# Which PSUM banks take the score maxima made first in a step: the two single banks instead of the pair

## The chip, the cores and the metric

The kernel runs on one core of a Trainium2 chip. The metric is the device time of one execution in microseconds (us). Engines are named as in the profile: PE (TensorE matmuls), PEld (TensorE weight loads), DVE (VectorE), ACT (ScalarE), POOL (GpSimd), SP (SyncE, which issues the DMAs).

## The reference

`x` is (8, 512, 1024). An attention block over the 512 channels (16 heads of 32, 1024 tokens, a mask over the keys from `cond_2048`) is followed by a linear layer on int8 values with one scale for each row, and the result is added to `x`:

```python
Q, K, V = (proj(Wq), proj(Wk), proj(Wv))          # einsum 'oc,bct->bto', then split into heads
att = einsum('bhqd,bhkd->bhqk', Q, K) / sqrt(32) + b[0]
att = softmax(att * m + (1 - m) * -1e30)          # m: mask of the keys
y = einsum('bhqk,bhkd->bhqd', att, V)             # back to (B, C, T)
scale = maximum(max(abs(y), axis=-1), 1e-7) / 127
q = clip(round(y / scale), -128, 127)             # int8
out = (q @ weight.T) * scale * w_scale + bias     # stored as float16
return x + out
```

All inputs but the int8 weight are float32.

## The kernel before, in words

The work is cut into 32 groups `i` (8 batches, 4 groups of 4 heads). A group is 16 steps: two halves of 512 queries, and in each half 8 blocks of 128 keys. So there are 512 steps `s`, with `t = s % 16`, after a prologue of 11 steps with negative numbers (`LEAD = 11`). The order of every engine's instructions is written out by hand (`tc.manual_schedule`); nothing is moved by a scheduler.

PSUM has eight banks of 512 float32 columns: four single ones, `one[0]` to `one[3]`, and two pairs, `two[0]` and `two[1]`, which an engine can read as 1024 columns in one instruction.

A step with `s >= 0` issues on PE, in this order:

1. `shift_scores(s)`, L338: four bf16 products that put minus the row maxima into the four banks of scores: two single banks and the pair `two[1]`. Even steps use `one[0]` and `one[1]`, odd steps `one[2]` and `one[3]`; from step 501 (`TAIL`) on it differs.
2. `scores(s, (0, 1))`, L348: the scores of heads 0 and 1, added to the single banks. Each head has 32 rows, so four heads can lie side by side on the array. The operands are float32, and a product is two passes.
3. `maxima(m, ..., (1, 0))`, L282, for step `m = s + 11`, that is 11 steps ahead: scores laid the other way round (128 queries by 512 keys), of which only the maximum over the keys is kept. Two heads are done in a step, each in two halves of the keys, so four products. The second half (`turn`) uses copies of q and k with neighbouring heads exchanged (`qt`, `kt`, made by DMA), so that the two halves of a head lie in two different row groups. Head 1 of the list is made first, head 0 second.
4. `scores(s, (2, 3))`, L348: the scores of heads 2 and 3, in `two[1]`.
5. In even steps `product` (L380): the exponentials of the last two steps times v, over the full height of the array, into the first single bank of this step's scores once the exponentials have been read from it. Its result is taken by ACT (L390) or DVE (L392).
6. The step's pieces of other work (`plan`): in even steps a 128-column piece of v for the next group (L186, kept by ACT, L267) in the second single bank of the scores; in odd steps two of a linear layer's half (kept by DVE, L525), a piece of q or k (kept by ACT, L220 and L222) and half a block of denominators (L398, kept by ACT, L405), one in each single bank of the scores. The last one is in the second bank.

`take_maxima` (L302) is DVE's part: it adds the mask row and takes the maximum, in one instruction over 1024 columns where a head's two halves lie in a pair, in two over 512 where they lie in two single banks; each is followed by the read of an accumulator (DVE_READ_ACCUMULATOR2, also L302). ACT turns the scores into exponentials (L362): two instructions for the single banks, one for the pair. POOL adds the exponentials up (L372).

`maxima_banks(s)` says which banks the two heads of the maxima get. For `s >= 0` these are the two single banks that the scores of this step do not use (so those that the step before filled with scores, then with its product and pieces, and that the next step's L338 writes), and the pair `two[0]`, which nothing else uses. The list's place 0 is head 0, its place 1 head 1; both `maxima` and `take_maxima` are called with `(1, 0)`, so place 1 comes first on PE and on DVE.

Of the kernel before, what the change touches and what calls it, by code (L numbers as in the profile page):

```python
# [33 lines left out]
def kernel(  # L34
# [44 lines left out]
    one = [psum.tile([P, HALF], F32, tag=f"one{a}", name=f"one{a}") for a in range(4)]  # L79
    two = [psum.tile([P, NH, HALF], F32, tag=f"two{a}", name=f"two{a}") for a in range(2)]  # L80

    def halves(t):
        return [t[:, a, :] for a in range(NH)]
# [5 lines left out]
    def maxima_banks(s):  # L89
        if s < 0:  # L90
            turns = (halves(two[0]), halves(two[1]), one[:2])
            return [turns[(2 * s + a) % 3] for a in range(2)]
        return [one[2:] if s % 2 == 0 else one[:2], halves(two[0])]

    x_sb = {}

# [611 lines left out]
    for s in range(-LEAD, n_steps):  # L708
# [36 lines left out]
        if s < 0:  # L745
            multiply()
            keep(False)
            maxima(m, maxima_banks(s))
            take_maxima(m, maxima_banks(s), range(2))
        else:  # L750

            shift_scores(s)
            scores(s, (0, 1))
            if m < n_steps:
                maxima(m, maxima_banks(s), (1, 0))
                take_maxima(m, maxima_banks(s), (1, 0))
            scores(s, (2, 3))
            exponentials(s)
            add_up(s)
            if s >= TAIL:  # L760
                for a in range(ON_ARRAY if s == TAIL + 1 else s - 1, s if s > TAIL else 0):
                    late(a)
            elif s > 0 and s % 2 == 0:
                acc = score_banks(s)[0][0]
                for a in (2, 1):
                    product(s - a, acc, a == 2, a == 1)
                keep_product((s - 2) // NT, (s - 2) % NT == 0, acc)
            multiply()
            keep(True)
# [68 lines left out]
```

## Time and profile before

| | |
|---|---|
| median of 3 runs | 2472.9 us (2472.07 to 2475.49) |
| the profiled execution | 2474.28 us, span 2472.5 us, mean granted clock 0.996 |
| PE busy | 2443.9 us, 99% |
| DVE busy | 1831.0 us, 74% |
| ACT busy | 1557.1 us, 63% |
| POOL busy | 2293.4 us, 93% |
| L282, products into `one` and into `two` | 2036 and 2060 passes, 589 ns each |
| L302 over 1024 columns | 515, 1225 ns each |
| L302 over 512 columns | 509 at 691 ns and 509 at 751 ns |
| one step in the middle | 4.81 us (even), 4.58 us (odd) |

The profile is one execution, with times in us from the start of the span. A matmul's end is modelled, so "busy" on PE covers passes that lie side by side, and also a step in which one of the row groups waits while another works. The list of waits names the waiting engine and line, then the one it waited for, with the total in us, the number of times and the longest.

### The profile page before, as it was taken

The numbers are of one execution on the slowest core, as the hardware profiler recorded it, in microseconds if no ns is written. First come the engines' busy times: TensorE is split into PE (matmuls) and PEld (weight loads), VectorE is DVE, ScalarE is ACT, GpSimd is POOL, SyncE is SP. The second block draws the span as 40 slices with busy tenths as digits, with TensorE's granted clock in tenths as the row PEclk, the third lists the DMA queues.
The fourth block names the chain that finished last, engine by engine and source line by source line (L and its number), as shares of the span: only waits on it lengthen the run. The fifth ranks groups of instructions, "written<-read, shape, count | busy, mean of one in ns | idle before, by whom it ended". The sixth has DMA issues, their size and how long they took to land.

```text
span 2472.5 us, 82389 instructions
## 1 busy us (share of the span) xinstructions
PE 2443.9 (99%) x35496; PEld 1156.9 (47%) x35496; DVE 1831.0 (74%) x3769; ACT 1557.1 (63%) x2382; POOL 2293.4 (93%) x961
## 2 busy tenths in 40 slices
PE   9999999999999999999999999999999999999987
PEld 4444444444444444444444444444444444444432
DVE  5677777777777777777777777777777777777774
ACT  1666666666666666666566676666665666666664
POOL 0999999999999999999999999999999999999992
PEclk9999999999999999999999999999999999999999
DMA  4013111121211211122111211112211122111111
GB/s 127 21 32 83 42 40 35 42 80 45 47 38 38 72 49 45 38 53 64 40 45 47 53 57 40 47 45 56 69 30 40 49 68 58 34 41 40 36 29 50
DMA packets 146590, 121.49 MB, mean 49 GB/s; under 512 B 77872, under 2 KB 111664, under 8 KB 146224
## 3 DMA queue, kind: packets, MB, share of 16 engines
q1 hardware_dynamic: 146224, 116.22, 17.8%
q8 instruction: 278, 4.55, 0.8%
q14 instruction: 88, 0.72, 0.1%
HBM read 57.70 MB, written 16.78 MB: 30 GB/s over the span
## 4 chain that ended last, share of the span: by engine, by line
PE 96%; DVE 2%; issue 0%; DMA 0%; ACT 0%; POOL 0%; SPq 0%; DVEq 0%; POOLq 0%
PE one L186 32%; PE one L380 19%; PE one L348 17%; PE one L282 17%; PE one L338 7%; PE one L398 3%; DVE rest L302 2%; PE two L282 1%; PE two L348 0%; DMA x<-in_x 0%; PE two L233 0%; PE two L559 0%; PE two L338 0%; ACT e L362 0%; PE one L233 0%
## 5 line engine op out<-in xcount | busy, mean ns | idle before, releaser
L372 POOL TENSOR_TENSOR sum<-sum,e 128x2048 f32<-128x2048 f32 x374 | 1707.8, 4566 | 22.1 <-ACT e L362 0.2
L302 DVE CUSTOM_DVE_ANT_0 rest<-two,row 128x1024 bf16<-128x1024 f32 x515 | 630.6, 1225 | 439.3 <-PE two L282 417.7
L362 ACT ACTIVATE e<-one,kbias 128x512 f32<-128x512 f32 x1024 | 648.9, 684 | 462.1 <-PE two L282 405.3
L362 ACT ACTIVATE e<-two,kbias 128x1024 f32<-128x1024 f32 x512 | 571.5, 1116 | 1.8 <-PE two L348 1.8
L348 PE MATMUL one<-qf,kf 32*128 32x512 f32 x2048 | 528.3, 589 | 0.0
L348 PE MATMUL two<-qf,kf 32*128 32x512 f32 x2048 | 526.7, 589 | 0.0
L282 PE MATMUL two<-kf,qf 32*128 32x512 f32 x1034 | 524.1, 589 | 0.3 <-DVE tops L302 0.3
L282 PE MATMUL one<-kf,qf 32*128 32x512 f32 x1022 | 521.3, 589 | 0.0
L282 PE MATMUL two<-kt,qt 32*128 32x512 f32 x1026 | 520.8, 590 | 0.0
L282 PE MATMUL one<-kt,qt 32*128 32x512 f32 x1014 | 517.4, 589 | 0.0
L380 PE MATMUL one<-e,v 128*32 128x512 f32 x4096 | 495.0, 599 | 0.0
L302 DVE CUSTOM_DVE_ANT_0 rest<-one,row,tops 128x512 bf16<-128x512 f32 x509 | 382.1, 751 | 75.3 <-DVE tops L302 2.0
L302 DVE CUSTOM_DVE_ANT_0 rest<-one,row 128x512 bf16<-128x512 f32 x509 | 351.5, 691 | 76.2 <-ACT qf L220 1.8
L372 POOL TENSOR_TENSOR sum<-e,e 128x2048 f32<-128x2048 f32 x63 | 286.6, 4549 | 84.9 <-ACT e L362 84.9
L186 PEld LDWEIGHTS one<-wv,x 128*32 128x32 f32 x8192 | 233.6, 110 | 151.9 <-issue 148.6
L380 PEld LDWEIGHTS one<-e,v 128*32 128x32 f32 x4096 | 107.8, 109 | 355.6 <-ACT e L362 198.2
L186 PE MATMUL one<-wv,x 128*32 128x128 f32 x8192 | 269.9, 273 | 0.0
L282 PEld LDWEIGHTS one<-kf,qf 32*128 32x128 f32 x1022 | 188.7, 185 | 120.6 <-issue 94.7
L186 PE MATMUL one<-x,wq 128*32 128x288 f32 (+2 forms) x4032 | 242.5, 381 | 0.5 <-ACT e L362 0.5
L186 PE MATMUL one<-x,wk 128*32 128x288 f32 (+2 forms) x3968 | 238.7, 381 | 0.0
L433 DVE RECIPROCAL den<-den 128x128 f32<-128x128 f32 x252 | 237.5, 945 | 0.3 <-ACT den L405 0.3
L282 PEld LDWEIGHTS one<-kt,qt 32*128 32x128 f32 x1014 | 187.0, 185 | 103.4 <-issue 49.6
(89 smaller groups left out, 2993.0 us busy)
## 6 DMA issues: line engine op xcount, KB each, us to landing
x<-in_x SPq DMA_DIRECT2D x32, 512.0 KB, 4.4
qt<-qf SPq DMA_DIRECT2D x256, 64.0 KB, 2.0
xr<-in_x SPq DMA_DIRECT2D x62, 256.0 KB, 3.2
out<-o SPq DMA_DIRECT2D x62, 256.0 KB, 2.2
wk<-in_wkT SPq DMA_DIRECT2D x32, 256.0 KB, 3.7
wq<-in_wqT SPq DMA_DIRECT2D x32, 256.0 KB, 4.1
kt<-kf SPq DMA_DIRECT2D x128, 64.0 KB, 2.0
mask<-in_cond SPq DMA_DIRECT2D x8, 512.0 KB, 4.6
```

The lines of the kernel that those rows point to most:

```text
L186: nc.tensor.matmul(acc[r : r + DH], weights[:, r : r + DH], moving, **kwargs)
L282: nc.tensor.matmul(accs[j][a], q[r : r + DH, n * P : (n + 1) * P], k[r : r + DH, :], start=True, stop=True,)
L302: nc.vector.tensor_tensor_reduce(out=rest[:, keys], in0=accs[j][a] if apart else both(accs[j]), in1=row[:, keys], scale=-1.0, scalar=top i ...
L338: nc.tensor.matmul(acc, ones_b[r, :], shift[r, :], start=True, stop=False)
L348: nc.tensor.matmul(accs[j], full[i, 1, kh][r, k0 * P : (k0 + 1) * P], full[i, 0, h][r, :], start=False, stop=True,)
L362: nc.scalar.activation(part, acc, AF.Exp, bias=kbias[:, kc : kc + 1], scale=SCALE)
L372: nc.gpsimd.tensor_tensor(sums[X], other, exps[s], ALU.add)
L380: nc.tensor.matmul(acc[r, :], v_sb[s // SG][:, kc, r], exps[s][:, j, :], start=start, stop=stop)
L398: nc.tensor.matmul(acc[j * DH : (j + 1) * DH, :], ones_f, term[:, j, :], start=start, stop=stop)
L433: nc.vector.reciprocal(d[:, cols], source[:, cols])
```

## The change

In `maxima_banks` the two entries of the list for `s >= 0` change places. Place 1, which is made first, now has the two single banks; place 0, made second, has the pair `two[0]`. `maxima` follows: the two products into single banks come first, those into the pair second. `take_maxima` follows too: DVE reads the two single banks first (512 and 512 columns), then the pair (1024 columns). Which heads, operands and row groups come first stays as it was, and so do the banks of the scores, products and pieces. The prologue's steps are not touched.

```diff
         if s < 0:
             turns = (halves(two[0]), halves(two[1]), one[:2])
             return [turns[(2 * s + a) % 3] for a in range(2)]
-        return [one[2:] if s % 2 == 0 else one[:2], halves(two[0])]
+        return [halves(two[0]), one[2:] if s % 2 == 0 else one[:2]]
```

## Prediction

> **What bounds the kernel now.** I read the engine totals and the chain of waits first, for the bound; then one step in the timeline; then the list of waits; then the groups of instructions for durations; last the granted clock by stage.
>
> ```profile
> PE 2443.9 (99%) x35496; PEld 1156.9 (47%) x35496; DVE 1831.0 (74%) x3769; ACT 1557.1 (63%) x2382; POOL 2293.4 (93%) x961
> ...
> PE 96%; DVE 2%; issue 0%; DMA 0%; ACT 0%; POOL 0%; SPq 0%; DVEq 0%; POOLq 0%
> ```
>
> TensorE is the bound: 96% of the chain that ended last. Whatever makes it wait in a step of about 4.7 us is paid in full; whatever makes VectorE shorter is worth only what TensorE waits for VectorE. Next, the start of one step (s = 203) in the timeline; columns are start, duration, engine, line, operation.
>
> ```profile
> 1009.17 0.39 PE L338 MATMUL one<-shift,ones_b 32*128 32x512 bf16 x2
> ...
> 1009.30 0.27 ACT L267 COPY v<-one 128x128 f32<-128x128 f32 x1 [0.29 <-PE one L186]
> ...
> 1009.39 0.59 PE L348 MATMUL one<-qf,kf 32*128 32x512 f32 x2
> ...
> 1009.40 0.59 PE L282 MATMUL two<-kt,qt 32*128 32x512 f32 x1
> ...
> 1009.82 0.18 PEld L282 LDWEIGHTS one<-kt,qt 32*128 32x128 f32 x1 [0.23 <-ACT v L267]
> ...
> 1010.25 0.59 PE L282 MATMUL one<-kt,qt 32*128 32x512 f32 x1
> ```
>
> Call the first L338 of a step time 0 (1009.17). Each L282 or L348 float32 product is two passes, 0.43 apart, in a group of 32 rows. Four products run side by side: two scores and the two maxima made first, with passes at 0.23 and 0.66; then the two maxima made second and two scores, at 1.09 and 1.52. Weights for the first maxima are loaded from 0.02 on, those for the second ones at 0.65 (1009.82). The ACT copy L267 of the previous step's last piece ends at 0.40. It empties one of the very banks `one` that the maxima use; today they are made second, so it is done 0.25 before their load. The 0.23 in brackets is no stall: the load stands where its row group came free, in steps with and without it.
>
> The nearest thing to the future wait is a step (s = 469) where a maximum made first waited for a DMA of `kt`:
>
> ```profile
> 2260.69 0.39 PE L338 MATMUL one<-shift,ones_b 32*128 32x512 bf16 x2
> ...
> 2261.18 0.29 PEld L282 LDWEIGHTS two<-kt,qt 32*128 32x128 f32 x2
> ...
> 2261.72 0.59 PE L282 MATMUL two<-kt,qt 32*128 32x512 f32 x1
> ...
> 2262.21 0.96 PE L348 MATMUL two<-qf,kf 32*128 32x512 f32 x2
> ...
> 2263.09 0.69 PE L186 MATMUL one<-x,wq 128*32 128x288 f32 x8
> ```
>
> The load came at 0.49, the second pass at 1.03 (0.54 after the load: the second load isn't hidden any more), the scores of that row group at 1.46 and 1.89 (2262.21 + 0.96 - 0.59), and the first full-height product at 2.40. In an undisturbed step that product starts at 2.07 to 2.08 (s = 202: 1006.44 against 1004.36). The step took 4.92 instead of 4.59. So one late row group costs: load time + 1.91 - 2.075 = load time - 0.165. Step 229 agrees: load at 0.25, step 4.67 instead of 4.59.
>
> **The change, part by part.** Nothing is added or removed. VectorE still reads 512, 512 and 1024 columns a step (0.69, 0.75 and 1.23 us), DMAs and evictions are the same, steps below 0 are untouched. Three things move, in the 501 steps from 0 to 500 that make maxima.
>
> *1. VectorE frees the single banks earlier.* The pair's read and its accumulator read (about 1.3 us) go behind the singles. The next step's L338 writes those singles first. What this is worth is in the list of waits (total us, times, longest):
>
> ```profile
> PE one L338 <- DVE tops L302: 11.5, 20, 2.2
> ```
>
> Twenty waits, 11.5 us in all, in the first 33 steps, a few in the middle and steps 490 to 500. In these VectorE ends up to 0.9 after time 0; 1.3 earlier is in time, so all 11.5 go. What is late next is the pair: its second use now begins with a load at 0.65 and a pass at 1.09, and VectorE's end stays where it was, so those steps have about as long as they need. I take -11.5; the least gain is 0, and there is no loss, since the same last end meets a load 0.65 later than L338.
>
> *2. The maxima in the single banks move from the load at 0.65 to the load at 0.02.* They must wait for the eviction of the previous step's pieces in the same two banks. Even steps end with a piece of v (L267); odd ones with 224 columns of q or k, or the denominators of 256 columns (L405), all in the second single bank, which takes the maximum of the turned heads.
>
> ```profile
> L267 ACT COPY v<-one 128x128 f32<-128x128 f32 x248 | 66.1, 267 | 184.9 <-PE one L186 183.5
> L405 ACT COPY den<-one 128x256 f32<-128x256 f32 x122 | 46.6, 382 | 1.0
> ...
> L220 ACT ACTIVATE qf<-one,top 128x224 f32<-128x224 f32 x61 | 27.3, 447 | 63.8 <-PE one L186 63.8
> L222 ACT COPY kf<-one 128x224 f32<-128x224 f32 x61 | 21.1, 346 | 63.8 <-PE one L186 63.8
> ```
>
> Each starts 0.13 after time 0 where ACT is free (it needs the last product's end, and that end and time 0 are tied together, so waiting earlier in the step doesn't bring it forward). Ends: v 0.40, k 0.48, q 0.58, denominators 0.51. From an ACT end to a TensorE load it takes 0.05 (the exponential of the first bank to the L380 load). So the cost is end + 0.05 - 0.165 = end - 0.115, and by the unrounded times end - 0.12: v 0.28, k 0.36, q 0.46, denominators 0.39. In two of the four places of the denominators ACT is late today (0.80 and 0.62, behind the quantising activations); the step before becomes 0.28 longer, which gives ACT that time back and leaves 0.52 and 0.53: 0.40 and 0.41.
>
> A group of 16 steps: 8 x 0.28 + 2 x 0.36 + 2 x 0.46 + 2 x 0.39 + 0.40 + 0.41 = 5.47 us. Of the 32 groups 31 have these pieces: 169.6 us. Queued behind the waiting load on TensorE are the maxima in the pair and the last two scores, whose row group ends the side-by-side part; so the full-height products wait, the next step too. ACT's exponentials of the first two banks do not: their scores stand ahead. VectorE reads the first single bank while the second is late, 0.77 us of cover.
>
> The first single bank is emptied by VectorE's sum (L392) or output scaling (L525) at 0.15 to 0.21 today; they fall to below 0 when the step before is 0.28 or more longer. Cost nothing; without that stretch 0.1 in 12 of 16 steps, but behind the other wait anyway.
>
> *3. The six DMA waits for kt* stand beside the new wait instead of alone: about 1.9 us of them are no longer extra.
>
> Sum: 169.6 - 11.5 - 1.9 = +156. The profiled run took 2474.3 (span 2472.5), which gives 2630.5; the median is 1.4 below that run: 2629.
>
> Bounds of one wait. From below: the L338 wait of step 10 (0.41) moved the end of its part by 0.40, with no hidden second load lost; with that, end + 0.05 - 0.23 - 0.04 (slack of the full-height product behind the exponential: 0.517 at least, 0.557 usually), 0.10 less each, 50 us less: 2580. From above: no slack (+0.04 each, 20), ACT not catching up (0.41 a group, 13), no VectorE gain (11.5): 2674. I take the middle row, since steps 229 and 469 are the same instruction, waiting at the same load.
>
> [...] The row here is the granted clock by stage:
>
> ```profile
> 45.00:90.00 45.00, 41.41 (x476) 19.20 (x476) 29.34 (x67) 19.29 (x30) 24.93 (x12) 0.92 0.24 56
> ...
> 160.00:2400.00 2240.00, 2231.90 (x33040) 1064.33 (x33036) 1694.12 (x3498) 1454.40 (x2226) 2177.67 (x893) 1.00 0.19 48
> ```
>
> The clock is 1.00 over a stretch that holds waits of 0.9 us in steps 490, 492 and 494. The new waits are half that and leave other row groups running, so I charge nothing.
>
> **The rivals.** *Faster:* the evictions turn out to be covered and only part 1 is left: 2472.9 - 11.5 = 2461. It decides if the last eviction ends before about 0.12 in the step. For it: VectorE is in 20 waits, the evictions in no real one. Against: every step's timeline has ACT ending at 0.40 or later. *No change,* 2473: the waits come, but the row groups overlap so that the late one hides; against it are steps 229 and 469, which paid. *Clock falls:* as in the 45 to 90 us row, 0.92, over 2240 us: another 195, 2825. That the change is not carried out is excluded: in the changed stream L282 writes `one` before `two` in each of these steps.
>
> **How the numbers follow.** Forecast and its bounds 0.92; much slower by the clock 0.03; no change 0.02; faster 0.03. The range leaves out the far ends of the bounds: 2600 to 2660. What a measurement can tell from no change is about 0.2%; faster beyond that 0.03, within it 0.02, slower 0.95.
>
> **What would show it.** Right: waits of L282 `one` for ACT v, den, qf and kf of 0.2 to 0.4 us in nearly every step; pairs of steps of 9.39 us grow to about 10.07; L338 waits for VectorE gone; TensorE still "busy" near 99%, because other row groups run; POOL's share falls. Wrong: step lengths unchanged with the L282 loads still late (the slack is larger than I read), or a clock below 1.00 in the middle.

## The result, and the profile after

The changed kernel takes 2635.4 us (median of 6 runs, 2631.3 to 2635.7) against 2473.8 us before (6 runs, 2472.1 to 2475.5): 1.065 times as long, 95% interval 1.0637 to 1.0664. The forecast for the median was 2629 us, a change of 156; the medians differ by 161.6. The profiled execution is the fastest of the six, 2631.28 us with a span of 2629.5; the sum in the prediction, made for the profiled execution, gave 2630.5.

The page of the changed kernel, engine totals and chain:

```profile
PE 2611.2 (99%) x35496; PEld 1358.8 (52%) x35496; DVE 1847.0 (70%) x3769; ACT 1584.0 (60%) x2382; POOL 2291.7 (87%) x961
...
PE 98%; DVE 1%; ACT 0%; issue 0%; POOL 0%; POOLq 0%; DVEq 0%; ACTq 0%
```

TensorE is still "99% busy", with the same number of products and 167 us more busy time. These totals don't show that one row group (32 rows of the array, `32*128` in the rows below) waits while others work. One step (s = 205, odd) in the timeline of the changed kernel does; columns are start, duration, engine, line, operation:

```profile
1081.01 0.39 PE L338 MATMUL one<-shift,ones_b 32*128 32x512 bf16 x2
...
1081.14 0.27 ACT L267 COPY v<-one 128x128 f32<-128x128 f32 x1 [0.59 <-PE one L186]
...
1081.46 0.29 PEld L282 LDWEIGHTS one<-kt,qt 32*128 32x128 f32 x2
...
1081.99 0.59 PE L282 MATMUL one<-kt,qt 32*128 32x512 f32 x1
...
1082.53 0.91 PE L348 MATMUL two<-qf,kf 32*128 32x512 f32 x2
...
1083.37 1.91 PE L186 MATMUL one<-x,wk 128*32 128x288 f32 x28
```

From the first L338: the copy of v ends at 0.40 (1081.14 + 0.27 - 1081.01), the first load of the turned maximum (L282 from `kt` and `qt`) stands at 0.45 instead of 0.02, its second pass at 0.98, the last score of that row group at 1.84 (1082.53 + 0.91 - 0.59), the first full-height product at 2.36 instead of 2.07 to 2.08. This is the picture of step 469 before, with ACT in the place of the DMA and 0.04 earlier. This step takes 4.87 us; the same one took 4.59 before.

How much longer each kind of step became, from L338 to L338, in the two traces (differences of medians over steps 33 to 479, so 27 or 28 of each kind):

| t of the step | which eviction it waits for | forecast, us longer | measured, us longer |
|---|---|---|---|
| odd | v | 0.28 | 0.28 to 0.29 |
| 0, 2 | k | 0.36 | 0.37 |
| 8, 10 | q | 0.46 | 0.47, 0.475 |
| 4, 6 | denominators | 0.39 | 0.39 |
| 12, 14 | denominators, ACT late before | 0.40, 0.41 | 0.39, 0.43 |
| 16 steps | | 5.47 | 5.58 |

The list of waits of the changed kernel (total us, times, longest) hides nearly all of this. Its first line here stands for the evictions, its second for the early release by VectorE:

```profile
PEld one L282 <- ACT qf L220: 13.5, 61, 0.3
...
PE one L338 <- DVE tops L302: 2.7, 3, 1.8
```

A wait is counted there as idle time of its engine; the weight loader is busy with second passes (of the scores and of the other maximum in the single banks) until 1081.42 in step 205, and the waiting load stands at 1081.46:

```profile
1081.23 0.19 PEld L348 LDWEIGHTS one<-qf,kf 32*128 32x128 f32 x2
1081.24 0.59 PE L282 MATMUL one<-kf,qf 32*128 32x512 f32 x1
1081.24 0.18 PEld L282 LDWEIGHTS one<-kf,qf 32*128 32x128 f32 x1
1081.46 0.29 PEld L282 LDWEIGHTS one<-kt,qt 32*128 32x128 f32 x2
1081.46 0.69 PE L282 MATMUL one<-kt,qt 32*128 32x512 f32 x1
```

The wait does show in the groups: the passes of the turned maximum have a mean of 641 ns instead of 589, since the first pass, which starts with its late load (both at 1081.46), is 0.69 long instead of 0.59.

```profile
L282 PE MATMUL one<-kt,qt 32*128 32x512 f32 x1014 | 569.3, 641 | 0.0
```

### The profile page after: what moved, and what is told of

Its sections match the earlier page's. It is cut to its first block, busy times and chain, and to the rows that moved or that the text cites. A ratio compares the mean times of both kernels' runs of the same rounds, so it can differ in the third digit from the quotient of the medians.

```text
span 2629.5 us, 82086 instructions
## 1 busy us (share of the span) xinstructions
PE 2611.2 (99%) x35496; PEld 1358.8 (52%) x35496; DVE 1847.0 (70%) x3769; ACT 1584.0 (60%) x2382; POOL 2291.7 (87%) x961
## 4 chain that ended last, share of the span: by engine, by line
PE 98%; DVE 1%; ACT 0%; issue 0%; POOL 0%; POOLq 0%; DVEq 0%; ACTq 0%
PE one L186 30%; PE one L380 18%; PE one L282 12%; PE two L348 12%; PE one L348 9%; PE two L282 7%; PE one L338 6%; PE one L398 3%; DVE rest L302 0%; PE two L233 0%; ACT e L362 0%; PE two L338 0%; PE one L231 0%; PE two L559 0%; PE one L233 0%
## 5 line engine op out<-in xcount | busy, mean ns | idle before, releaser
L348 PE MATMUL two<-qf,kf 32*128 32x512 f32 x2048 | 694.2, 587 | 0.0
L282 PE MATMUL one<-kt,qt 32*128 32x512 f32 x1014 | 569.3, 641 | 0.0
L282 PE MATMUL one<-kf,qf 32*128 32x512 f32 x1022 | 531.0, 599 | 0.4 <-ACT den L405 0.4
L282 PE MATMUL two<-kf,qf 32*128 32x512 f32 x1034 | 524.2, 589 | 0.2 <-DVE tops L302 0.2
L282 PE MATMUL two<-kt,qt 32*128 32x512 f32 x1026 | 520.1, 589 | 0.0
L348 PEld LDWEIGHTS two<-qf,kf 32*128 32x128 f32 x2048 | 322.2, 185 | 131.5 <-issue 58.4
L267 ACT COPY v<-one 128x128 f32<-128x128 f32 (+1 forms) x252 | 67.5, 268 | 250.4 <-PE one L186 250.3
```

Of the source, the lines that this page charges most:

```text
L267: nc.scalar.copy(v_sb[i][:, keys, :].rearrange("p k c -> p (k c)"), acc)
L282: nc.tensor.matmul(accs[j][a], q[r : r + DH, n * P : (n + 1) * P], k[r : r + DH, :], start=True, stop=True,)
L348: nc.tensor.matmul(accs[j], full[i, 1, kh][r, k0 * P : (k0 + 1) * P], full[i, 0, h][r, :], start=False, stop=True,)
```

## The experiments

The theory is that of the prediction: the maxima made first wait for the evictions of the step before in the single banks. The rival is that the order of the banks or of VectorE's reads costs time in itself, whatever is evicted. Each time is compared with runs of the kernel before that were made beside it on the same chip, as a ratio with its 95% interval in brackets.

### Leaving the evictions out

Both kernels without ACT's copies of v, q, k and the denominators, from the second or third group on; the functions that keep a piece return early and name the first groups' tiles instead, so the kernel works on with old values.

```diff
     def keep_project(i, which, h, cols, acc):
+        if i >= 2:
+            full[i, which, h] = full[1, which, h]
+            turned[i, which] = turned[1, which]
+            return
...
     def keep_v(i, keys, acc):
+        if i >= 1:
+            v_sb[i] = v_sb[0]
+            return
...
     def keep_denominators(X, cols, acc):
+        if 2 <= X < n_halves - 4:
+            dens[X] = dens[X % 2]
+            return
```

The control, on the kernel before:

> The kernel before, where ACT's copies of the pieces of v (from the second group on), q and k (from the third group on, with their DMAs of turned heads) and the denominators (of halves 2 to 59) are left out; later groups use the first groups' tiles, and the products themselves stay. Control for the next run. Theory and rival alike: those copies lie beside TensorE's work and end before anything waits for them: 2474 us, 2468 to 2476.

Measured: 2470.1 us, 0.9984 (0.9974 to 0.9993) of the kernel before, whose median beside it was 2473.8. Most of the small gain of 3.7 us is in the steps with t = 5, which lose 2.85 us in all between steps 33 and 479: the DMAs of `kt`, which went with the copies, were what six of them waited for.

On the changed kernel:

> The changed kernel with the same copies left out. Theory (the waits are for these evictions): the 170 us of waits vanish and the 11 us of VectorE's early release stay; what is left are VectorE's sum and output scaling in the first single bank, at 0.15 to 0.21 in the step, 0.03 to 0.1 us each: the control minus 10 to plus 14 us, 2463 to 2488. Rival (order of banks or reads in itself, or a lower clock): 2635 us as with the copies.

Measured: 2477.8 us, 1.0014 (1.0005 to 1.0024) of the kernel before, 7.7 us above the control. So 154 of the 162 us are gone with the copies, while the order of banks and reads is that of the change. The rival is out for all but these 7.7 us. They fit what was expected of VectorE's evictions (L392 and L525 in the first single bank), without being shown to be that: steps with t = 1, 2, 5, 7, 8, 9, 10, 13 and 15 are 0.02 to 0.07 longer than the control's, the others 0.00 to 0.01. The steps with t = 3 and 11, which follow a product that ACT takes instead of VectorE, are among the others. The list of waits of this run shows VectorE's early release by itself:

```profile
PE one L345 <- DVE tops L309: 3.7, 4, 2.5
```

L345 is L338 here, seven lines further down; the control has 11.9 us, 21 times.

### One eviction made longer

Each piece of v, from the third group on, copied twice.

```diff
-        nc.scalar.copy(v_sb[i][:, keys, :].rearrange("p k c -> p (k c)"), acc)
+        for _ in range(2 if i >= 2 else 1):
+            nc.scalar.copy(v_sb[i][:, keys, :].rearrange("p k c -> p (k c)"), acc)
```

On the kernel before:

> The kernel before, where each piece of v from the third group on is copied twice out of its bank by ACT (the same values). Control for the next run. Theory: the second copy ends at about 0.67 in the step; the load of the maxima in the single banks, made second, moves from 0.66 to at most 0.75 and its pass at 1.09 does not: 2474 us, 2472 to 2480. Rival (more ACT work alone is what costs): as much more as in the next run.

Measured: 2472.6 us, 0.9995 (0.9985 to 1.0004). No cost of the extra copies can be seen there.

On the changed kernel:

> The changed kernel with each piece of v from the third group on copied twice. Theory: the wait in each of about 240 odd steps grows by one copy, 0.27 to 0.29 us: 65 to 70 us more than the changed kernel, 2702 us, 2690 to 2712. Rival (waits are not for this eviction): 2635 us.

Measured: 2703.3 us, 1.0926 (1.0910 to 1.0943), 68 us above the changed kernel. Every odd step grew by 0.296 (medians of two traces), even ones by 0.00. The timeline of this run, with line numbers one higher:

```profile
1109.71 0.39 PE L339 MATMUL one<-shift,ones_b 32*128 32x512 bf16 x2
...
1109.85 0.56 ACT L268 COPY v<-one 128x128 f32<-128x128 f32 x2 [0.59 <-PE one L186]
...
1110.46 0.18 PEld L283 LDWEIGHTS one<-kt,qt 32*128 32x128 f32 x1 [0.33 <-ACT v L268]
```

Two copies end at 0.70, the load stands at 0.75. Only now does the loader sit idle before it, and the wait gets its name.

### The change in odd or in even steps alone

```diff
+        singles = one[2:] if s % 2 == 0 else one[:2]
+        if s % 2 == 1:  # in the other run: s % 2 == 0
+            return [halves(two[0]), singles]
+        return [singles, halves(two[0])]
```

> The change is made in odd steps only (those that follow an even step, whose last eviction is a piece of v). Theory (waits for the eviction): about 250 waits at 0.28 to 0.29 us each, 71 us, less the L338 waits that follow odd steps (about 9 us) and less about 2 us where the kt wait stands beside: 2534 us, 2526 to 2545. Rival (the order of banks or of VectorE's reads costs something in itself, whatever is evicted): half of the 161.6 us of the whole change, 2555 us.

Measured: 2534.9 us, 1.0243 (1.0226 to 1.0260). Odd steps are 0.28 to 0.29 longer, even ones 0.00.

> The change is made in even steps only (those that follow an odd step, whose last eviction is k, q or the denominators). Theory: 0.37, 0.39, 0.39, 0.475, 0.475 as in the changed kernel's steps 2, 4, 6, 8 and 10 of sixteen, 0.37 in step 0, but 0.68 and 0.50 in steps 12 and 14, because ACT, late there with the quantising activations, gets no longer steps before them: 3.65 us a group of 16, 31 groups, 113 us: 2587 us, 2575 to 2595. Without that last effect (0.40 and 0.43): 2576 us. Rival (bank or read order in itself): half of 161.6, 2555 us.

Measured: 2579.7 us, 1.0425 (1.0409 to 1.0440). Even steps cost 0.36 (t = 0, 2), 0.39 (4, 6), 0.46 (8, 10), 0.68 (12) and 0.54 (14, where 0.50 was expected); odd ones 0.00. Step 12 costs 0.68 here and 0.39 in the full change: ACT's delay with the quantising activations is paid when the step before isn't longer. That part of the sum had only been argued; here it is shown. Of the two parts, 60 and 105 us, neither is half of the whole, as the rival had it.

### One order without the other

TensorE's order changed, VectorE's as before: `take_maxima(m, maxima_banks(s), (0, 1))` instead of `(1, 0)` in the changed kernel.

> TensorE makes the maxima in the single banks first, as changed, but VectorE reads the pair first, as before. Theory: the waits for evictions stay (about 160 us), and VectorE's chain of about 2.9 us starts at 2.27 in the step, when the pair is complete, not at 1.41; it ends at about 5.2 with the single banks, which the next step's L338 writes. Odd steps take 4.87, so each L338 after them waits about 0.35 us more, some 88 us; after even steps of 5.2 little: 2720 us, 2660 to 2770. Rival (the read order by itself is what cost time in the change): back towards 2474 us.

Measured: 2689.8 us, 1.087 (1.0854 to 1.0887). VectorE's reads begin at 2.15 to 2.4 in the step and end at 5.0 to 5.3. So their new place in the change saves 54 us against this, and isn't what costs the time. The extra cost was expected to be 85 us, about 0.35 in every odd step; it is 0.41 at t = 5 and 13, 0.14 to 0.16 at 1, 7 and 15, and at most 0.04 at 3, 9 and 11.

VectorE's order changed, TensorE's as before: the same edit in the kernel before.

> TensorE makes the maxima in the pair first, as before, but VectorE reads the single banks first, as changed. Theory: no wait for evictions; VectorE's chain starts at 2.27 in the step, when the single banks are complete, and ends with the pair at about 5.2; the next step's first load of the pair stands at 0.02, so in the steps after the short ones (4.58 us) it waits until about 0.67, 0.5 us of cost; after those steps, now 5.3 us long, none: about 250 times 0.5, 126 us: 2600 us, 2570 to 2650. Rival (the read order by itself is what cost time in the change): 2635 us with waits of the kind seen in the changed kernel, L282 one for ACT.

Measured: 2556.4 us, 1.033 (1.0315 to 1.0346). That is below the range expected. The mechanism holds, in even steps alone, but the size was missed by a third, 0.32 to 0.35 us a step (0.42 at t = 6) instead of 0.5. The timeline of this run, an odd step's end and the even step after it:

```profile
1036.96 1.22 DVE L302 CUSTOM_DVE_ANT_0 rest<-two,row 128x1024 bf16<-128x1024 f32 x1
...
1037.75 0.39 PE L338 MATMUL one<-shift,ones_b 32*128 32x512 bf16 x2
...
1038.11 0.08 DVE L302 DVE_READ_ACCUMULATOR2_ANT tops<- 128x1 f32 x1
1038.24 0.18 PEld L282 LDWEIGHTS two<-kf,qf 32*128 32x128 f32 x1
```

The load of the pair stands at 0.49, not 0.67: VectorE's reads began at 2.14 in the step and ended at 5.00, where 2.27 and 5.2 had been put down. With load time - 0.165 the cost is 0.325. So the start and the length of VectorE's chain were mis-sized, and the rule for the cost of a late load, taken from a wait for a DMA, also holds for a wait for VectorE.

### The change where VectorE was late

The change in 14 steps, six of them between 489 and 497.

```diff
+        singles = one[2:] if s % 2 == 0 else one[:2]
+        if s in (0, 1, 7, 15, 17, 23, 25, 31, 489, 491, 493, 495, 496, 497):
+            return [halves(two[0]), singles]
+        return [singles, halves(two[0])]
```

> The change only in 14 steps whose following step's L338 waited for VectorE in the kernel before (0, 1, 7, 15, 17, 23, 25, 31, and eight between 489 and 497). Theory: each such wait of 0.5 to 0.9 us goes and 0.28 us for the eviction of v comes: about 0.4 us each, 4 to 6 us: 2469 us, 2466 to 2473. Rival (the change costs in itself wherever it is made): 2474 us or a little more.

Measured: 2471.9 us, 0.9992 (0.9983 to 1.0001). This can't be told from no change, and the gain expected is not shown. The trace says where it went. The waits for VectorE at L338 fall as meant:

```profile
PE one L341 <- DVE tops L305: 3.3, 3, 2.5
```

(L338 here is L341; 11.5 us before.) But a chosen step such as 7 costs 0.28 as expected, and step 8 gets back 0.42, not the 0.64 that its wait had cost: it makes the pair first again, and its loads now wait for the pair that VectorE read last. They stand at 0.38, which costs 0.22 by the rule. That wait (L282 `two` for VectorE) goes from 2.8 to 5.0 us. In steps 489 to 496 the sum is 0.00 us, for the same reason: the odd steps there are only 2.9 to 3.4 us long, VectorE's reads end at 4.3 to 4.6 after their start, and the first loads of the pair in the next step, which is not changed, stand at 1.0 to 1.6. No version that does all the work was shown to beat the kernel before.

## Why the prediction was right

The mechanism was right for the evictions, which are nearly the whole change, and so was the price of one late load. The sum was some 5 us short; that it met the profiled execution within 1 us is luck.

**Bound.** TensorE is the bound and the waits were paid in full: the spans differ by 157.0 us, the steps by 159.1.

**The wait for the evictions**, 169.6 us forecast. The model of one late row group, load time - 0.165, taken from two waits for a DMA, gave each kind of step to within 0.02. The four other waits of this kind in the trace before, which the prediction didn't use, agree: steps 85, 389, 245 and 165 have the late load at 0.36, 0.81, 0.85 and 1.11 and are 0.19, 0.64, 0.68 and 0.94 us longer than others of their kind. What the term missed is 0.11 a group or 3.4 us: 0.06 in the odd steps (0.287 each, put down as 0.28) and 0.05 in the steps that wait for q and k, whose evictions end 0.01 later than before (q at 0.59 instead of 0.58). That these waits are the cause is shown from three sides: leaving the copies out, making one longer, and the change in one half of the steps at a time.

**VectorE's early release**, -11.5 forecast. L338's waits for VectorE fall from 11.5 to 2.7 us. But the term was the total of a list of waits, taken as if a wait that loses its cause is worth its length in the list, and the steps show something else. The listed waits lie in steps 0 to 32 and 490 to 500, none in the middle. Steps 0 to 32 grew by 4.3 us, where the costs in the table would add up to 11.5: 7.2 came in, though the list lost only 3.0 there. (Steps 8 and 16 before, for example, have 0.3 in the list and are 0.64 longer than others of their kind.) Steps 490 to 500 grew by 0.3 us instead of 3.9; 1.6 of that difference is the clock (below), so 2.0 came in, though the list lost 5.8. There VectorE is later still, and the wait for it comes back at L282: in step 490 its reads of the step before end at 1.00, its output scaling (L525), which empties the first single bank, ends at 1.39, and the first maximum's load stands at 1.45. By this estimate, which counts in whatever else these steps gained, the term is -9.2, so the forecast took off 2.3 too much.

**The six waits for kt**, -1.9 forecast: between steps 33 and 479 the steps with t = 5 grew by 5.2 us in all, where 28 times 0.281 would be 7.9. So 2.7 us lie beside each other.

With these sizes the sum is 173.0 - 9.2 - 2.7 = 161.1, against 161.6 between the medians.

**Why the profiled execution was nearer.** The traces show the granted clock at about half speed for two stretches of 3.4 us near the end of the profiled kernel before, from 2396.8 (0.51) and from 2458.3 (0.50). The profiled execution of the changed kernel has neither: 1.00 from 2400 to 2620. The first stretch falls into step 498, which takes 7.30 us there and 5.66 in the two controls on the kernel before (no copies, v twice), whose clock is 1.00 in that step; the time after the last L338 is 26.8 us before and 25.1 in the changed kernel. So about 3.3 us of the 4.6 by which the profiled pair differs less than the medians are the clock near the end.

**What was said of the other engines** held: the exponentials of the first two banks don't move (they start at 1.34 in step 205 before and after), the granted clock doesn't fall, POOL's share drops from 93 to 87%, even and odd step together take 10.07 us (5.20 + 4.87 at t = 4 and 5).

```profile
160.00:2400.00 2240.00, 2240.00 (x31044) 1181.88 (x31040) 1596.00 (x3266) 1383.91 (x2086) 2031.07 (x836) 1.00 0.17 46
```

This row of the busy times by stage has the window, its length, the busy times of PE, PEld, DVE, ACT and POOL with their instructions, and then the granted clock: 1.00, as before, with a late load of one row group in each of the some 445 steps of this window, 0.28 to 0.48 us of cost each. The prediction charged nothing for the clock, and nothing was paid. The clock as a rival is out.

**Wrong in form:** the sign by which it was to be known, waits of L282 `one` for ACT in nearly every step of the list of waits. They are in every step of the timeline, but hardly any are in the list.

**Left open:** the other five runs of the changed kernel are 3 to 4 us longer than the profiled one. Their mean granted clock was 0.996 or 0.997 against 0.998, which fits half-speed stretches near the end as in the kernel before, but there is no trace of one of them, so this is not shown.

## What to carry to other kernels

When an accumulator bank changes its place in a step, look up when its last reader ends and when its next writer's weights are loaded; here the first 0.4 to 0.6 us of each step, in which other products had covered the evictions, were worth 6.5%. Look for a rare stall of the same instruction in the trace you have: two steps out of 512 gave the price of one late load, and with it that of nearly the whole change. Don't take the length of a wait in the list for the time that its end brings: the first 33 steps gained more than twice what the list lost there, steps 490 to 500 about a third of it. Where row groups work side by side, read step lengths and timelines; engine totals and the list of waits hardly showed here that one of them was late.

## What the runs showed of the hardware that had not been expected

VectorE's three reads of a step take 2.86 us, from 2.14 to 5.00, when TensorE makes the pair first and VectorE reads it last. Between the two single banks 0.15 us pass, but the pair follows 0.05 after the second one's end (1036.16 + 0.75, then 1036.96); in the changed kernel 0.16 pass there too (step 205: the second read from 1083.21 for 0.75, the pair's from 1084.12). What makes this difference is not shown. The early start and the short gap are part of what made the forecast for the changed read order alone too high.

Whether a wait gets into the list depended here on what else its engine did. With one copy of v, about 250 waits at the load left 0.2 us in the list under ACT's v; with two copies, 0.3 us longer each, they left 77.9:

```profile
L283 PEld LDWEIGHTS one<-kt,qt 32*128 32x128 f32 x1014 | 148.6, 183 | 105.7 <-ACT v L268 77.9 <-ACT qf L220 12.7 <-DVE tops L303 0.6
```
